# The last batch of a two-layer attention kernel: output products moved earlier, a flag tested earlier, a ScalarE table loaded earlier

## The chip, the cores and the metric

The kernel runs on one core of a Trainium2 chip. The core has five engines that run their own instruction streams and meet through semaphores: TensorE (PE in the profile, with its weight loads listed apart as PEld), VectorE (DVE), ScalarE (ACT), GpSimd (POOL) and SyncE (SP), which here issues most DMA transfers. The metric is device time in microseconds. All data are 32-bit floats; in the profile one 128x512 product of this kernel shows as two rows, each a weight load and a matmul.

## The reference, cut to what matters

The input x has shape 8 x 512 x 32 x 32: eight batches, 512 channels, 1024 positions. Two layers follow, each of the form "x plus attention of the group-normalised x". The change lies in the second layer, and almost all of it in its eighth and last batch:

```python
attn = jnp.einsum('bhdq,bhdT->bhqT', q, k) * scale
attn = jnp.einsum('gh,bhqT->bgqT', w_head, attn)      # mix the 8 heads
attn = jax.nn.softmax(attn, axis=-1)
attn = (attn - mean) / jnp.sqrt(var + EPS)            # over the whole map
attn = attn * in_gamma[None, :, None, None] + in_beta[None, :, None, None]
out = jnp.einsum('bhqT,bhdT->bhqd', attn, v)
out = out.reshape(b, t, c)
out = out @ w_proj.T + b_proj
```

## The kernel before, in words

**Second layer, one batch.** The class `Attention1` works through 8 blocks of 128 positions. `scores` (L1630) multiplies queries and keys into PSUM and ScalarE copies the result to `raw` (L1642). `regroup` (L1648, on SP's queue) moves `raw` into `re_t` by DMA so that the heads lie beside each other. `mix` (L1667) multiplies by the head weights into two PSUM tiles, and ScalarE takes the exponential of each (L1680). `flip` (L1695, VectorE) transposes it, `moments` (L1709, VectorE) takes the sums, and `values` (L1725) multiplies by the values. `leave` (L1741, ScalarE) copies the result into `out_view`, which has four blocks of 128 channels (`NCH` is 4), each made of two position blocks' results. `totals` (L1763 to L1783) gives the softmax divisors, which go through DRAM and come back spread over partitions as `rzb`; `divide` (L1810) multiplies a block by them. Blocks 0, 1 and 2 are divided by GpSimd during the steps, block 3 by VectorE in the tail.

**Order.** The order on PE, ACT, DVE, POOL and SP is written out by hand: inside `manual_schedule`, each engine runs its instructions in the order of the Python calls. `step(p, t, ag)` interleaves the work of block p (scores), p-1 (mix, flip) and p-2 (values). `ag` is an `Agenda`: a list of functions, each with a slot number, run when `step` reaches that slot. In the ninth step (p = 8, t = 0 to 3) no new scores are made. Slot 31.5 (`4 * NT - 0.5`) comes after the values and the copy of block 6's first half and just before `mix(7, 0)`.

**PSUM.** The pool `ps_m` has three tiles of two banks, used by scores, mixes and, in the tail, by the output products (`m_psum`); `ps_a` has two tiles of one bank (`acc_psum`).

**The tail.** After the ninth step `values(7, 0)` is finished, `values(7, 1)` follows, then `totals(3)`, `broadcast`, `instance` (variance terms of the normalisation) and `out1_last`. That function computes, for four output chunks `oc` of 128 channels and two halves `f` of 512 positions, the sum over four blocks `n` of weights times `out_view` (L1552; 32 products of 128x512 in all). For chunks 0 to 2 the blocks 0 to 2 come first and block 3 later; chunk 3 is done whole at the end (L1603). Between them stand `instance_end` (L1835 to L1847: scale A and offset cv), `divide(3)`, `check` (L1796 to L1803), the offset product (L1578), its sum `off` (L1582) and 32 ScalarE additions of `off` to x (L1589). Each output tile is then `ys = psum * A` (L1608), `ys + x` (L1613), and a DMA to DRAM (L1614).

**The flag.** At the very end VectorE reduces `chk` (L2024 to L2029), a matmul sums over partitions into `pflag` (L2031), VectorE compares and writes `flag` (L2033, L2034). Every engine loads the flag (L2038) and branches (L2039): if a softmax sum was out of range, the whole computation is run again in a general form (`general_path`); with these inputs the branch is taken past it. After that the engines meet and the program ends (L2088).

**The start.** ScalarE's first function is used at L864, where chunks 1 and 3 of the first batch are normalised (chunks 0 and 2 by VectorE, L862). The first products (L904) read these chunks.

Of the kernel before, what the change touches and what calls it, by code (L numbers as in the profile page):

```python
# [18 lines left out]
P = 128  # L19
# [5 lines left out]
Z_MAX, RZ_MAX = 1e17, 1e10  # L25
# [442 lines left out]
def tile_two_attention_layers(  # L468
# [47 lines left out]
    def const_tile(name, shape, dt=F32):  # L516
        return const.tile(shape, dt, tag=name, name=name)
# [751 lines left out]
    with ExitStack() as l1:  # L1269
# [10 lines left out]
        NCH = NT // 2  # L1280

        def acc_psum(nm):
            return ps_a.tile([P, FB], F32, tag="a", name=nm)
# [4 lines left out]
        def small_psum1(nm):  # L1288
            return m_psum(nm)[:, 0]
# [210 lines left out]
        def out_view(b):  # L1500


            return qo_t[b].rearrange("p (n two) a t -> p n (two a t)", two=2)
# [36 lines left out]
        def out1_last(a):  # L1540


            b = a.b
            w = w_t["p", b]
            tiles = {}

            def products(oc, blocks):
                if oc not in tiles:
                    tiles[oc] = m_psum(f"pp1_{b}_{oc}")
                for f in range(NFB):  # L1550
                    for n in blocks:
                        nc.tensor.matmul(  # L1552
                            tiles[oc][:, f], w[:, n, ts(oc, P)], out_view(b)[:, n, ts(f, FB)],
                            start=(n == 0), stop=(n == NCH - 1),
                        )

            last = NCH - 1

            x = rawpool.tile([P, NCC, T], F32, tag="raw", name="xs_last")
            for oc in range(NCC):  # L1560
                nc.sync.dma_start(out=x[:, oc], in_=x1_d[b][ts(oc, P), :])
            wsum = epool.tile([P, 2 * T], F32, tag="e", name="wsum")[:, :C]
            ys = etpool.tile([P, NCC, NFB, FB], F32, tag="et", name="ys_last")
            small = acc_psum("small_last")
            off = stat.tile([P, NCC, H], F32, tag="off", name="off", bufs=1)
            for oc in range(3):
                products(oc, range(last))
                if oc == 0:
                    nc.vector.tensor_add(wsum, w[:, 0], w[:, 1])
                    for n in range(2, NCH):  # L1570
                        nc.vector.tensor_add(wsum, wsum, w[:, n])
                    a.instance_end(small)
                    a.divide(last)
                    a.check()
                if oc == 1:
                    pc = small[:, H : H + NCC * H]
                    for o in range(NCC):
                        nc.tensor.matmul(  # L1578
                            pc[:, o * H : o * H + H], wsum[:, ts(o, P)], a.cv,
                            start=True, stop=True,  # L1580
                        )
                    nc.vector.tensor_add(  # L1582
                        off, pc.rearrange("p (c g) -> p c g", g=H),
                        pb1.unsqueeze(2).to_broadcast([P, NCC, H]),
                    )
                    for o in range(NCC):
                        for g in range(H):
                            xg = x[:, o, ts(g, P)]
                            nc.scalar.activation(  # L1589
                                xg, xg, AF.Identity, bias=off[:, o, g : g + 1]  # L1590
                            )
            halves = [acc_psum(f"pp1_last_{f}") for f in range(NFB)]
            h = FB // P
            for oc in range(NCC):
                if oc < last:
                    products(oc, [last])
                for f in range(NFB):
                    if oc < last:
                        ps = tiles[oc][:, f]
                    else:  # L1600
                        ps = halves[f]
                        for n in range(NCH):
                            nc.tensor.matmul(  # L1603
                                ps, w[:, n, ts(oc, P)], out_view(b)[:, n, ts(f, FB)],
                                start=(n == 0), stop=(n == NCH - 1),
                            )
                    y = ys[:, oc, f]
                    nc.vector.tensor_mul(  # L1608
                        y.rearrange("p (g t) -> p g t", t=P),
                        ps.rearrange("p (g t) -> p g t", t=P),  # L1610
                        a.A[:, f * h : f * h + h].unsqueeze(2).to_broadcast([P, h, P]),
                    )
                    nc.vector.tensor_add(y, x[:, oc, ts(f, FB)], y)  # L1613
                    nc.sync.dma_start(out=out_d[b, ts(oc, P), ts(f, FB)], in_=y)  # L1614

        class Attention1:
            def __init__(self, b):
# [239 lines left out]
            def step(self, p, t, ag):  # L1857
# [84 lines left out]
        for b in range(B):  # L1942
# [81 lines left out]
        nc.vector.tensor_reduce(top[:, 0:1], chk[:, 0], AX.X, ALU.max)  # L2024
        nc.vector.tensor_reduce(top[:, 1:2], chk[:, 1], AX.X, ALU.max)
        nc.vector.tensor_scalar(top[:, 0:1], top[:, 0:1], RZ_MAX, None, ALU.is_lt)
        nc.vector.tensor_scalar(top[:, 1:2], top[:, 1:2], Z_MAX, None, ALU.is_lt)
        good = stat.tile([P, 1], F32, tag="good", name="good")
        nc.vector.tensor_mul(good, top[:, 0:1], top[:, 1:2])  # L2029
        pf = small_psum1("pflag")  # L2030
        nc.tensor.matmul(pf[:, 0:1], ones, good, start=True, stop=True)  # L2031
        bad = stat.tile([P, 1], F32, tag="bad", name="bad")
        nc.vector.tensor_scalar(bad, pf[:, 0:1], P - 0.5, None, ALU.is_lt)  # L2033
        nc.vector.tensor_copy(flag, bad)  # L2034

    both.close()
    ordered.close()
# [54 lines left out]
```

## Time and profile before

| What | us |
|---|---|
| median of 3 runs | 3967.3 (3964.85 to 3968.17) |
| the profiled execution's own time | 3964.89 |
| its span, first to last instruction | 3963.1 |
| last `values(7, 1)` products begin (L1725) | 3913.68 |
| last output product row begins (L1603) | 3948.81 |
| last output sum ends (L1613) | 3950.92 |
| flag written (L2034) | 3952.46 |

PE is busy 98% of the span, DVE 70%, ACT 50%, POOL 4%. Times in the views are counted from the span's start. A line of a view names the code line, the engine, the operation, output <- input by tile name, and in brackets the idle time before it and what ended that. In a table of stretches each engine has its busy time and its number of instructions; PEclk is the share of full speed that PE's clock was granted.

### The profile page before, as it was taken

The page shows a single profiled execution, that of the slowest core. Times are in us where ns is not written, and L with a number is a line of the kernel's source. Part 1 is how long each engine was busy: PE and PEld are TensorE (multiplying, and loading weights), DVE is VectorE, ACT ScalarE, POOL GpSimd, SP SyncE. Part 2 cuts the span into 40 slices and gives each one's busy share as a digit, 9 for nine tenths or more (in the row PEclk, how much of TensorE's full clock was granted, in tenths as well). Part 3 has the DMA queues.
Part 4 walks back from the last instruction along what each step waited for, and adds up shares of the span by engine and source line. Part 5 has one row for each costly group of instructions (what it writes and reads, how often), then busy time and mean ns, then how long its engine had stood idle before and what let it go on. Part 6 is the DMA issues. An engine that isn't in the chain of part 4 may idle for free.

```text
span 3963.1 us, 95453 instructions
## 1 busy us (share of the span) xinstructions
PE 3874.9 (98%) x41868; PEld 1823.7 (46%) x41868; DVE 2769.6 (70%) x3741; ACT 1971.4 (50%) x2431; POOL 141.2 (4%) x182
## 2 busy tenths in 40 slices
PE   8999999999999999999999999999999999999997
PEld 4353535344353535344544545545545445445454
DVE  4747475665757474856967958859768679588596
ACT  1726354453627172624716718538347267175284
POOL 0000000000000000000100100001001001000010
PEclk9999999999999999999999999999999999999998
DMA  3313131121121121216938839749568478397494
GB/s 121 123 48 117 47 118 46 55 73 65 55 72 68 61 76 48 89 49 173 230 114 208 211 104 237 198 119 236 158 158 220 134 192 226 98 229 191 124 226 124
DMA packets 249593, 519.09 MB, mean 131 GB/s; under 512 B 51024, under 2 KB 58192, under 8 KB 242512
## 3 DMA queue, kind: packets, MB, share of 16 engines
q1 hardware_dynamic: 241984, 500.08, 44.2%
q0 software_dynamic: 7184, 12.81, 1.5%
q8 instruction: 331, 5.42, 0.6%
q14 instruction: 94, 0.77, 0.1%
HBM read 197.16 MB, written 46.92 MB: 62 GB/s over the span
## 4 chain that ended last, share of the span: by engine, by line
PE 90%; DVE 5%; DMA 3%; ACT 1%; issue 1%; SPq 0%; ACTq 0%; DVEq 0%
PE s L1086 11%; PE a L1112 11%; PE a L1725 11%; PE s L1630 10%; PE m L1667 6%; PE pk_p L904 6%; PE pq_p L904 5%; PE pv L1456 5%; PE pv_p L904 5%; PE pp_p L904 5%; PE pq L1381 4%; PE pp L1381 4%; PE pk L1381 3%; DMA re<-raw 3%; DVE et L1695 1%; DVE bn L1709 1%
## 5 line engine op out<-in xcount | busy, mean ns | idle before, releaser
L1695 DVE STREAM_TRANSPOSE et<-e 128x2048 f32<-128x2048 f32 x256 | 589.5, 2303 | 100.0 <-ACT e L1680 99.0
L1725 PEld LDWEIGHTS a<-et,v 128*64 128x64 f32 x16384 | 510.8, 139 | 296.4 <-issue 273.4
L1709 DVE BATCH_NORM_STATS2 bn<-e 128x6 f32<-128x512 f32 x1024 | 635.1, 681 | 0.0
L1091 ACT ACTIVATE e<-s 128x1024 f32<-128x1024 f32 x512 | 497.2, 1026 | 233.8 <-PE s L1086 233.4
L1642 ACT COPY raw<-s 128x1024 f32<-128x1024 f32 x480 | 470.2, 1018 | 211.6 <-PE s L1630 179.0
L1680 ACT ACTIVATE e<-m 128x1024 f32<-128x1024 f32 x512 | 496.3, 1021 | 156.1 <-issue 56.3
L1725 PE MATMUL a<-et,v 128*64 128x64 f32 x16384 | 558.9, 225 | 11.2 <-DVE et L1695 7.8
L1099 DVE TENSOR_TENSOR zacc<-zacc,e 128x1024 f32<-128x1024 f32 x384 | 468.7, 1221 | 87.8 <-ACT e L1091 65.5
L1630 PE MATMUL s<-k,q 64*64 64x512 f32 x4096 | 515.2, 607 | 5.8 <-DVE q L1496 3.2
L1086 PE MATMUL s<-q,k 64*64 64x512 f32 x4096 | 490.1, 593 | 2.3 <-ACT e L1091 2.3
L1112 PE MATMUL a<-e,v 64*64 64x512 f32 x4096 | 484.1, 589 | 0.0
L1667 PE MATMUL m<-re,wmix 32*32 32x512 f32 x8192 | 311.0, 602 | 19.5 <-DMA re<-raw 16.5
L1112 PEld LDWEIGHTS a<-e,v 64*64 64x64 f32 x4096 | 156.7, 133 | 282.8 <-issue 282.2
L1086 PEld LDWEIGHTS s<-q,k 64*64 64x64 f32 x4096 | 147.9, 133 | 275.2 <-issue 240.5
L1630 PEld LDWEIGHTS s<-k,q 64*64 64x64 f32 x4096 | 127.8, 132 | 220.8 <-issue 87.1
L1456 PE MATMUL pv<-wv,y 128*128 128x512 f32 x480 | 214.3, 599 | 0.0
L1773 POOL DMA_DIRECT2D zd<-rz x96 | 52.5, 552 | 3508.2 <-DVE rz L1767 3506.0
L1741 ACT COPY q<-a 64x256 f32<-64x256 f32 x256 | 94.0, 367 | 148.3 <-PE a L1725 146.2
L1456 PEld LDWEIGHTS pv<-wv,y 128*128 128x128 f32 x480 | 88.6, 190 | 119.8 <-issue 106.5
L1667 PEld LDWEIGHTS m<-re,wmix 32*32 32x32 f32 x8192 | 68.8, 103 | 162.4 <-ACT raw L1642 69.3
L1462 DVE COPY v<-pv 128x512 f32<-128x512 f32 x30 | 20.7, 689 | 159.5 <-PE pv L1456 80.9
L1097 DVE TENSOR_TENSOR zacc<-e,e 128x1024 f32<-128x1024 f32 x64 | 78.3, 1223 | 55.9 <-ACT e L1091 55.9
(317 smaller groups left out, 3866.4 us busy)
## 6 DMA issues: line engine op xcount, KB each, us to landing
re<-raw SPq DMA_DIRECT2D x1024, 256.0 KB
left_q<-left_q SPq DMA_DIRECT2D x17, 1792.0 KB
left_p<-left_p SPq DMA_DIRECT2D x17, 1792.0 KB
left_k<-left_k SPq DMA_DIRECT2D x10, 1792.0 KB
x<-in_x_dram SPq DMA_DIRECT2D x32, 512.0 KB
rzb<-zd SPq DMA_DIRECT2D x128, 128.0 KB
x<-x SPq DMA_DIRECT2D x64, 256.0 KB
y<-x SPq DMA_DIRECT2D x32, 512.0 KB
```

The lines of the kernel that those rows point to most:

```text
L904: nc.tensor.matmul(out, st, mv, start=start, stop=(k == 1), skip_group_check=True)
L1086: nc.tensor.matmul(ps[c * D : c * D + D, m], k[r, hp, k0 : k0 + D], q[r, hp, ts(f, FB)], start=True, stop=True,)
L1091: nc.scalar.activation(e[i], ps, AF.Exp, scale=S0 * S0)
L1112: nc.tensor.matmul(acc[g][a][m * D : m * D + D], v[rows, kc, ts(2 * hp + m, D)], e[i][rows, m], start=(kc == 0), stop=(kc == NG - 1),)
L1456: nc.tensor.matmul(ps[:, m], y_t[b][:, c, ts(2 * i + m, P)], w[:, c], start=(c == 0), stop=(c == NCC - 1),)
L1630: nc.tensor.matmul(ps[c * D : c * D + D, m], qo_t[b][r, p, hp, ts(c, D)], k_t[b][r, hp, ts(kh, FB)], start=True, stop=True,)
L1642: nc.scalar.copy(dst, ps)
L1667: nc.tensor.matmul(ps[a // 2][c * 32 : c * 32 + 32, a % 2].rearrange("p (r h k) -> p h r k", r=2, h=2), wmix[rows].rearrange("p g i -> p ( ...
L1680: nc.scalar.activation(e[:, :, 2 * h : 2 * h + 2].rearrange("p r a k -> p a r k"), ps[h].rearrange("p a (r k) -> p a r k", r=2), AF.Exp,)
L1695: nc.vector.transpose(self.et[p, u].rearrange("p kb (r st a) g q -> p st kb r (a g q)", r=2, st=2)[:, st], self.e[p, s].rearrange("p r a ( ...
L1709: nc.vector.bn_stats(self.bn[n][:, p % 2, s, a], e[:, :, a].rearrange("p r k -> p k r"))
L1725: nc.tensor.matmul(acc[two * D : two * D + D, s].rearrange("p (x q) -> p x q", q=4), v_t[b][:, kb, ts(g, D)], et[:, kb, :, g], start=(kb = ...
```

## The change

Three edits:

1. `out1_last` is cut in two. It now returns `products` and `rest`. A function `prelude` in slot 31.5 of the last batch calls it and runs `products(0, [0, 1])`: four 128x512 products. After `leave(7, 0)`, ahead of `values(7, 1)`, come `products(0, [2])` and `products(1, [0, 1])`: six more. `products` skips what has been done. The rest of the tail keeps its order, without these ten products.
2. The test of the sums becomes `set_flag`, called after `off` and the products of chunk 2's first three blocks, ahead of the last results. Its matmul writes to the tile `small_last` in place of one from `ps_m`. In the built program SP's load of the flag stands ahead of the eight output transfers; on the other engines it stays after their last work.
3. A one-column ScalarE `Identity` into a new tile `first_act` stands early in the program, so ScalarE's table load comes before L864. The tile takes 32 bytes of each partition ahead of `chk`, so in the built program all SBUF tiles allocated later lie 32 bytes higher.

```diff
+    first_act = const_tile("first_act", [P, 1])
+    nc.scalar.activation(first_act, ones[:, :1], AF.Identity)
     chk = const_tile("chk", [P, 2, NCHK])
...
-            tiles = {}
+            tiles, done = {}, set()
             def products(oc, blocks):
+                blocks = [n for n in blocks if (oc, n) not in done]
+                done.update((oc, n) for n in blocks)
                 if oc not in tiles:
                     tiles[oc] = m_psum(f"pp1_{b}_{oc}")
...
+            def rest():
...
+                for oc in range(3):
+                    products(oc, range(last))
...
+                set_flag(small)
+                halves = [acc_psum(f"pp1_last_{f}") for f in range(NFB)]
...
+            return products, rest
...
+        def set_flag(pf):
+            top = stat.tile([P, 2], F32, tag="top", name="top")
+            nc.vector.tensor_reduce(top[:, 0:1], chk[:, 0], AX.X, ALU.max)
+            nc.vector.tensor_reduce(top[:, 1:2], chk[:, 1], AX.X, ALU.max)
+            nc.vector.tensor_scalar(top[:, 0:1], top[:, 0:1], RZ_MAX, None, ALU.is_lt)
+            nc.vector.tensor_scalar(top[:, 1:2], top[:, 1:2], Z_MAX, None, ALU.is_lt)
+            good = stat.tile([P, 1], F32, tag="good", name="good")
+            nc.vector.tensor_mul(good, top[:, 0:1], top[:, 1:2])
+            nc.tensor.matmul(pf[:, 0:1], ones, good, start=True, stop=True)
+            bad = stat.tile([P, 1], F32, tag="bad", name="bad")
+            nc.vector.tensor_scalar(bad, pf[:, 0:1], P - 0.5, None, ALU.is_lt)
+            nc.vector.tensor_copy(flag, bad)
...
+                def prelude():
+                    out_products.extend(out1_last(a))
+                    out_products[0](0, [0, 1])
+                out_products = []
+                ag.at(4 * NT - 0.5, prelude)
...
                 a.values(last, 0, 2, 3)
                 a.leave(last, 0)
+                out_products[0](0, [2])
+                out_products[0](1, [0, 1])
                 a.values(last, 1, 0, 1, 2, 3)
                 a.leave(last, 1)
                 a.totals(NCH - 1)
                 a.broadcast(1)
                 a.instance()
-                out1_last(a)
+                out_products[1]()
...
-        top = stat.tile([P, 2], F32, tag="top", name="top")
...
-        pf = small_psum1("pflag")
-        nc.tensor.matmul(pf[:, 0:1], ones, good, start=True, stop=True)
```

More of the change, by code (lines that the diff above doesn't have):

```diff
@@ L1557, in out1_last @@
             last = NCH - 1
[L1559 to L1580, printed above, removed]
-                        )
[L1582 to L1597, printed above, removed]
-                    if oc < last:
[L1599 to L1614, printed above, removed]
+            def rest():
+                x = rawpool.tile([P, NCC, T], F32, tag="raw", name="xs_last")
+                for oc in range(NCC):
+                    nc.sync.dma_start(out=x[:, oc], in_=x1_d[b][ts(oc, P), :])
+                wsum = epool.tile([P, 2 * T], F32, tag="e", name="wsum")[:, :C]
+                ys = etpool.tile([P, NCC, NFB, FB], F32, tag="et", name="ys_last")
+                small = acc_psum("small_last")
+                off = stat.tile([P, NCC, H], F32, tag="off", name="off", bufs=1)
+                for oc in range(3):
+                    products(oc, range(last))
+                    if oc == 0:
+                        nc.vector.tensor_add(wsum, w[:, 0], w[:, 1])
+                        for n in range(2, NCH):
+                            nc.vector.tensor_add(wsum, wsum, w[:, n])
+                        a.instance_end(small)
+                        a.divide(last)
+                        a.check()
+                    if oc == 1:
+                        pc = small[:, H : H + NCC * H]
+                        for o in range(NCC):
+                            nc.tensor.matmul(
+                                pc[:, o * H : o * H + H], wsum[:, ts(o, P)], a.cv,
+                                start=True, stop=True,
+                            )
+                        nc.vector.tensor_add(
+                            off, pc.rearrange("p (c g) -> p c g", g=H),
+                            pb1.unsqueeze(2).to_broadcast([P, NCC, H]),
+                        )
+                        for o in range(NCC):
+                            for g in range(H):
+                                xg = x[:, o, ts(g, P)]
+                                nc.scalar.activation(
+                                    xg, xg, AF.Identity, bias=off[:, o, g : g + 1]
+                                )
+                set_flag(small)
+                halves = [acc_psum(f"pp1_last_{f}") for f in range(NFB)]
+                h = FB // P
+                for oc in range(NCC):
+                    if oc < last:
+                        products(oc, [last])
+                    for f in range(NFB):
+                        if oc < last:
+                            ps = tiles[oc][:, f]
+                        else:
+                            ps = halves[f]
+                            for n in range(NCH):
+                                nc.tensor.matmul(
+                                    ps, w[:, n, ts(oc, P)], out_view(b)[:, n, ts(f, FB)],
+                                    start=(n == 0), stop=(n == NCH - 1),
+                                )
+                        y = ys[:, oc, f]
+                        nc.vector.tensor_mul(
+                            y.rearrange("p (g t) -> p g t", t=P),
+                            ps.rearrange("p (g t) -> p g t", t=P),
+                            a.A[:, f * h : f * h + h].unsqueeze(2).to_broadcast([P, h, P]),
+                        )
+                        nc.vector.tensor_add(y, x[:, oc, ts(f, FB)], y)
+                        nc.sync.dma_start(out=out_d[b, ts(oc, P), ts(f, FB)], in_=y)
@@ L2021, in tile_two_attention_layers @@
             q_projection(b + 1).run()
-        top = stat.tile([P, 2], F32, tag="top", name="top")
[L2024 to L2029, printed above, removed]
-        pf = small_psum1("pflag")
-        nc.tensor.matmul(pf[:, 0:1], ones, good, start=True, stop=True)
-        bad = stat.tile([P, 1], F32, tag="bad", name="bad")
-        nc.vector.tensor_scalar(bad, pf[:, 0:1], P - 0.5, None, ALU.is_lt)
-        nc.vector.tensor_copy(flag, bad)
     both.close()
```

## The prediction

> **What bounds the kernel now.** PE is busy 98% of the span, so I read the chain of work that ended last first, for the last 50 us. Columns: start, length, what.
>
> ```profile
> 3913.68 6.23 PE a L1725 x128
> ...
> 3920.33 5.35 PE pp L1552 x12
> ...
> 3932.13 10.40 PE pp L1552 x24
> 3942.53 6.88 PE pp_last L1603 x16
> ...
> 3950.23 0.69 DVE ys_last L1613
> ...
> 3952.31 0.15 DVE flag L2034
> ```
>
> From 3913.68 to 3949.4 PE is the chain; then come the last output sum and the test of the flag. Next, where PE stands still before that (timeline; in brackets the idle time and what ended it):
>
> ```profile
> 3894.01 1.34 PE L1667 MATMUL m<-re,wmix 32*32 32x512 f32 x32 [3.82 <-DMA re<-raw]
> ...
> 3913.68 6.23 PE L1725 MATMUL a<-et,v 128*64 128x64 f32 x128 [5.34 <-DVE et L1695]
> ```
>
> Two holes, 3.82 and 5.34 us. The second is VectorE's: from 3897.40 it flips and sums without a pause until 3916.2. The 128 products after it take 6.23 us, while 128 of the same kind from 3904.38 take 3.95. The stretches tell why (stretch, length, PE, PEld, DVE, ACT, POOL busy, PEclk):
>
> ```profile
> 3894.85:3898.26 3.41, 3.41 (x80) 2.06 (x64) 0.86 (x1) 1.94 (x2) 0.00 (x0) 0.50 0.73 194
> 3898.26:3908.40 10.14, 10.07 (x317) 7.53 (x288) 10.14 (x11) 6.04 (x8) 0.00 (x0) 1.00 0.01 3
> ...
> 3911.92:3918.74 6.82, 5.06 (x95) 5.09 (x97) 4.25 (x6) 0.00 (x0) 0.00 (x0) 0.50 0.01 2
> ```
>
> After each hole PE's clock is halved, in steps of 3.41 us. Last, the code lines of the flag's branch and of the end:
>
> ```profile
> L2039 POOLq EVENT_SEMAPHORE  x5: 17/43/43, 3956.3 to 3956.6; - x5
> L2039 PEldq COMPARE_BRANCH  x1: 4335/4335/4335, 3953.1 to 3953.1; - x1
> L2039 DVEq EVENT_SEMAPHORE  x1: 21/21/21, 3956.6 to 3956.6; - x1
> L2039 POOLq INC_SWDGE_SEM  x1: 1237/1237/1237, 3956.7 to 3956.7; - x1
> L2088 POOLq DRAIN  x3: 46/103/4315, 3957.9 to 3962.8; - x3
> ```
>
> The flag is written at 3952.46, each engine loads it (0.5 us) and branches at 3953.1; then 3.2 us pass before POOL goes on, 3.5 before DVE, 4.3 for PE. POOL then does 1.24 us and a drain of 4.32, until 3962.26; the engines meet and the span ends at 3963.1. From the last sum's end (call it A, 3950.92) to the end are 12.2 us.
>
> [...] worked out from the matmul records, windows in which PE was busy 25, 42, 46 and 49% were followed by half clock, those with 50 and 59% not. [...]
>
> **Part 1: ten products moved.** A row of a 128x512 product takes 0.429 us (15 rows from 3942.37 to 3948.81), a product two rows.
>
> Prelude: 4 products are 8 rows, 3.43 us. PE comes free at 3890.20 and the mix's data come at 3894.0, so it ends at 3893.7: hidden, with 0.3 us to spare. The weights and blocks 0 and 1 have long been there (last division of block 1: 3849.8 to 3852.1); its PSUM tile was freed at 3887.2. If the cover were gone, 3.43 us would fall on the mix and VectorE's run. The window is now over half busy, so the mix runs at full clock: 1.15 instead of 1.34 us. VectorE's run, which starts when its exponentials are done, moves 0.2 us ahead.
>
> The prelude keeps one of three `ps_m` tiles. So each later mix waits for both exponentials of the mix before: mix 1 at 3897.2 (before 3897.19), mix 2 at 3900.4 (3899.85), mix 3 at 3904.0 (3903.21). Queued behind them on PE are the values. The exponentials of mixes 2 and 3 wait for VectorE's sums (to 3901.9 and 3906.5), so the run isn't delayed: cost 0. PE's holes there are below 1 us in each window. Values(7,0) ends at 4.0+1.15+3.95 past 3900: 3909.1 instead of 3908.33.
>
> Six products: 12 rows, 5.15 us, to 3914.3. VectorE's last flip ends at 3913.35, so values(7,1) starts 0.6 us later than before, but at full clock: 3.95 instead of 6.23. With the divisors' 0.55 us PE is done at 3918.75, not 3920.33: 1.58 gained.
>
> Tail: what is late next is VectorE. Before, PE had 5.35 us of products while VectorE made `isb`; now nothing. `isb` takes 2.40 us from there (3920.33 to 3922.73): 3921.15. Then PE: `instance_end` 0.35, two products 1.72, to 3923.3. VectorE has the weights' sum ahead (2.1 us, to 3923.2), then 2.99 us to `cv`: 3926.25. So PE stands 2.4 and 2.95 us. Then 8 offset rows 0.79; 12 rows 5.15; the flag's matmul 0.2; 12 rows 5.15, to 3937.6; the last of 16 rows starts 6.44 later, 3944.05, and A follows as before (3948.81 to 3950.92) after 2.1: 3946.15. So A comes 4.77 us earlier. Division 3 waits for `rzb`, 8.8 us behind the divisors: 3927.9 to 3929.1, ahead of its use at 3932.5. `off` then waits for `check`, to 3930.0; ScalarE's 9.45 us end at 3939.9, its first chunk at 3932.8, in time for the sums from 3934.2.
>
> The two holes in the tail can halve the clock. Sliding the 3.41 us window over them: in some 60% of positions a window under half busy leaves the next halved, 1.7 us lost; in the others nothing. Mean 1.0. Before, the hole of 5.34 lost 2.5 us in this profile (5.06 us at half clock), and 1.7 as a mean over positions: so 0.8 of the gain is this profile's.
>
> **Part 2: the flag.** VectorE's 7 short operations (1.5 us with waits) leave the end; in their new place five end by 3930.9, inside its idle time, and the last two wait for PE at 3932.5, ahead of the first output at 3933.5. SP loads the flag ahead of the eight output DMAs (0.48+0.19+0.03, to 3934.0); its first DMA is due at 3934.9. POOL has nothing left to do, so its load, fetch, 1.24 us and drain of 4.32, 10 us in all, lie under the products. ACT's lie there too. Then DVE ends last: its queue runs ahead of its data path (the step for L1571's second sum stands at 3923.4, while the first, begun at 3923.4, runs 0.69), so it loads the flag during the last sum: A-0.6, +0.55, +0.08, +3.47 is A+3.5, then SP's and POOL's meeting, 1.15: A+4.65. If it loads only after the sum: A+5.4. PE, whose last row starts at A-2.1, needs 0.5+4.4: A+2.8. The last output landed 1.7 us after A. So 12.2 becomes 4.65 to 5.4: 6.8 to 7.5 gained; I take 7.3.
>
> **Part 3: the table.** It saves ScalarE 1.28 us ahead of chunk 1. But see:
>
> ```profile
> 20.65 8.84 PE L904 MATMUL pk_p<-n,left_k 128*128 128x512 f32 x16 [4.39 <-DVE n L862]
> 21.00 2.37 ACT L864 ACTIVATE n<-x,nn,scale 128x1024 f32<-128x1024 f32 x2
> ...
> 24.37 0.59 ACT L928 COPY tmp<-pk_p 128x512 f32<-128x512 f32 x1 [1.00 <-PE pk_p L904]
> 26.09 0.59 ACT L928 COPY tmp<-pk_p 128x512 f32<-128x512 f32 x1 [1.13 <-PE pk_p L904]
> ```
>
> PE starts on VectorE's chunk 0; four rows end at 24.3 (3.7 us), the next four take 1.72: the first are at half clock, two of them cover 20.65 to 22.36, and chunk 1 is there at 22.19. From there PE runs without a hole to 33 us. Worth 0 to 0.2; without that cover 1.2. I take 0.1.
>
> **Sum.** 4.77+7.3+0.1-1.0 = 11.2 against the profile's 3964.9: 3953.7. The runs' median is 2.4 above it; from there, without this profile's 0.8, 3967.3-10.4 = 3956.9. I take 3956.
>
> **Rivals.**
> (a) The end doesn't shrink: POOL's drain of 4.32 us waits for the others and starts after them. For it: nothing else in the trace ends with it. Against: its start at 3957.95 follows POOL's own step directly, and it outlasts SP's last step (3958.67). Then the flag's 1.55 is all of part 2: 5.5 us less gain, 3961.5.
> (b) The clock takes the gain: holes of 2.4 and 2.95 us, plus short ones between the mixes, halve two or three windows, 3.4 to 5.1 us instead of 1.0. Against: PE is over 65% busy in every mix window. 3958.5 to 3960.
> (c) Slower: the 32 bytes. [...] The chain has 3% of the span, 119 us, in `re<-raw` transfers[...]. It decides from 9% (10.7 us); to be slower by 0.2% it needs 16%, giving 3975. Against: PE waits for these transfers only 15 times, 16.5 us.
>
> **Chances.** Forecast 0.72, (a) 0.12, (b) 0.10, (c) 0.06. A measurement of this kernel can tell about 0.2%, 7.9 us, from no change: 3959.4. Forecast and half of (b) are faster, 0.77; (a) and the rest 0.17 the same; (c) 0.06 slower. Range 3951 to 3961.5: below by a tail without lost windows and a table worth 1.2, above by (b) and up to (a); (c) is left out.
>
> **What would show it.** Right: prelude rows between 3890.2 and 3893.7 with the mix near 3894.0; values(7,1) in about 3.95 us; two PE holes of 2 to 3 us in the tail, ended by `isb` and `icv`; POOL's drain over before the last outputs; last sum to end of span 4.6 to 5.4 us; PE's first row still at 20.65. Wrong: the mix late by the prelude, the drain after DVE's branch, or a changed duration in the rows that the change doesn't touch.

## The result, and the profile after

The changed kernel takes 3956.1 us (median of 22 runs, 3949.9 to 3966.3), the kernel before 3965.2 us in the runs beside it (22, 3959.1 to 3969.3). The ratio is 0.9981, 95% interval 0.9975 to 0.9987: 7.5 us less, 5.2 to 9.9 (the two medians lie 9.1 us apart, within that interval). It is faster, by about as much as can be told from no change. The profiled execution took 3957.81 us, its span is 3956.0 us. (The line numbers of the tail are 4 to 9 higher than before, those of the end 19.)

The chain of work that ended last, its last part (start, length, what):

```profile
3912.11 5.35 PE pp L1556 x12
3917.46 3.88 PE a L1734 x128
...
3924.09 0.69 DVE wsum L1575
...
3929.17 1.30 PE small_last L1584 x8
3930.47 6.69 PE pp L1556 x12
...
3942.54 6.88 PE pp_last L1610 x16
...
3950.24 0.69 DVE ys_last L1620
```

The products now stand ahead of the last values, which take 3.88 us, and the flag has left the end of the chain. In the middle the chain has gone over to VectorE (from the divisors at 3921.8 to `icv` at 3929.1). The twelve product rows after that take 6.69 us, where the twelve at 3912.11 take 5.35.

PE's holes, from the timeline (in brackets the idle time and what ended it):

```profile
3892.90 3.70 PE L1556 MATMUL pp<-q,left_p 128*128 128x512 f32 x8
3896.98 1.15 PE L1676 MATMUL m<-re,wmix 32*32 32x512 f32 x32 [0.38 <-DMA re<-raw]
...
3912.04 5.42 PE L1556 MATMUL pp<-q,left_p 128*128 128x512 f32 x12
3917.39 3.95 PE L1734 MATMUL a<-et,v 128*64 128x64 f32 x128
...
3924.32 0.36 PE L1844 MATMUL small_last<-isb,ones 64*128 64x8 f32 x2 [2.54 <-DVE isb L1835]
...
3929.17 1.30 PE L1584 MATMUL small_last<-icv,wsum 128*128 128x8 f32 x8 [2.59 <-DVE icv L1856]
```

The prelude fills the first hole but for 0.38 us, and the mix still starts when its data come. The hole of 5.34 us ahead of the last values is gone. Two holes stand in the tail instead. The stretches of the clock's 3.41 us around the second (stretch, length, busy time and count of PE, PEld, DVE, ACT and POOL, PEclk, DMA share, GB/s):

```profile
3926.42:3929.83 3.41, 0.82 (x7) 0.66 (x6) 2.29 (x15) 0.00 (x0) 0.00 (x0) 1.00 0.77 185
3929.83:3933.24 3.41, 3.41 (x8) 1.86 (x8) 2.37 (x10) 0.14 (x1) 0.00 (x0) 0.50 0.99 374
```

PE was busy for 0.82 of 3.41 us, and the next 3.41 us ran at half clock: this is the only such stretch in the last 2000 us of the changed kernel's profile ahead of the end; the one before had three there, one of them of 6.83 us.

The code lines of the flag's branch and of the end:

```profile
L2058 POOLq COMPARE_BRANCH  x1: 50/50/50, 3938.3 to 3938.3; - x1
L2058 POOLq INC_SWDGE_SEM  x1: 1232/1232/1232, 3941.2 to 3941.2; - x1
L2058 PEldq COMPARE_BRANCH  x1: 3992/3992/3992, 3942.3 to 3942.3; - x1
L2058 DVEq COMPARE_BRANCH  x1: 76/76/76, 3950.9 to 3950.9; - x1
L2058 DVEq EVENT_SEMAPHORE  x1: 21/21/21, 3954.1 to 3954.1; - x1
L2107 POOLq DRAIN  x3: 46/103/4315, 3942.5 to 3955.7; - x3
```

POOL branches at 3938.3, and its drain of 4.32 us runs from 3942.5 to 3946.8, under the products. The fetch that the prediction counts for POOL is the time from its branch to its next step: 3.2 us before (3953.07 to 3956.26), 2.6 here (3938.26 to 3940.82). The instruction queues moved 5 packets (0.05 MB) from 3953 to 3956.5 before, and 4 (0.03 MB) from 3938 to 3942.5 here; that they set its length isn't shown. DVE still branches at the last output sum's end (A, 3950.93), and goes on 3.2 us later; SP branches at 3951.3, behind its last output transfer. From A to the end of the span are 5.1 us instead of 12.2.

Three distances split the last 60 us so that they can be compared between profiles whatever came earlier: from the start of the mix, `mix(7, 0)`, to the end of the divisors' last product (z), from z to A, and from A to the end. The starts, ends and clock records come from each kernel's trace:

| Kernel | mix to z | z to A | A to end | half clock after z |
|---|---|---|---|---|
| before | 26.32 | 30.60 | 12.2 | 0 |
| flag only | 27.44 | 30.82 | 4.8 | 0 |
| table only | 26.19 | 30.60 | 12.6 | 0 |
| changed | 24.80 | 29.15 | 5.1 | 3.41 |
| changed, again | 24.80 | 30.55 | 5.1 | 10.24 |
| products only | 24.82 | 27.25 | 12.5 | 3.41 |
| products only, again | 24.80 | 30.69 | 12.3 | 10.24 |
| changed, GpSimd late | 24.80 | 29.92 | 10.3 | 10.24 |
| changed, prelude twice | 24.81 | 30.81 | 4.8 | 10.24 |
| changed, with filler | 24.80 | 27.48 | 5.2 | 0 |
| prelude only | 26.50 | 28.05 | 5.3 | 0 |
| six only | 24.80 | 31.08 | 4.9 | 6.83 |
| other order of the tail | 24.80 | 24.36 | 4.8 | 0 |
| other order, ScalarE's share | 24.80 | 23.08 | 4.9 | 0 |

### The profile page after: what moved, and what is told of

The parts are those of the page before. It is cut to its first block, busy times and chain, and to the rows that moved or that the text cites. A ratio compares the mean times of both kernels' runs of the same rounds, so it can differ in the third digit from the quotient of the medians.

```text
span 3956.0 us, 95453 instructions
## 1 busy us (share of the span) xinstructions
PE 3873.6 (98%) x41868; PEld 1820.5 (46%) x41868; DVE 2770.1 (70%) x3741; ACT 1970.7 (50%) x2432; POOL 140.9 (4%) x182
## 3 DMA queue, kind: packets, MB, share of 16 engines
q8 instruction: 331, 5.42, 0.6%
```

## The experiments

Runs of one kernel scatter by 3 us (standard deviation) before the change and by 4 us after it, so a ratio from some 20 runs has an interval of about 2.5 us to each side. Effects of 1 to 2 us are read in the table above, and the ratios only say whether the sum agrees.

### The flag alone

The kernel before, with the removed block at the end turned into `set_flag` and called here:

```diff
+            set_flag(small)
             halves = [acc_psum(f"pp1_last_{f}") for f in range(NFB)]
```

> The kernel before with the flag's test alone moved ahead of the last results (in the tile small_last); no products moved, no early table load. Theory (the end shrinks because every engine's load of the flag and its branch, POOL's drain above all, lie under the products): last output sum to end of span 4.6 to 5.4 us instead of 12.2, the tail's products unchanged but for one matmul of 0.2 us (PE free before the mix to last output sum 60.7 to 61.0 us), so 7.0 us less, ratio about 0.9982. Rival (most of what the changed kernel gains comes from the products, the flag gives only its own 1.55 us): ratio 0.9996.

Measured: 0.9982 (0.9975 to 0.9988, 21 runs), 7.1 us less. A to the end is 4.8 us. PE free to A (from PE's last values ahead of the mix to the last output sum) is 62.25 us (3884.77 to 3947.02), 1.25 more than the upper value expected. z to A is unchanged (30.82 against 30.60), so the excess lies ahead of z: in this profile two stretches of 6.83 us at half clock fell there, against 3.41 and 6.83 before. The flag is worth what the theory says; the rival's 1.55 us is out. Its 7.1 us are also as much as the runs show for the whole change (7.5 us, and 6.7 in a second comparison below): that the ten products add to it has to be read from the stages.

### The products alone, twice

The changed kernel with the flag's test put back to the end and `first_act` taken out:

```diff
-    first_act = const_tile("first_act", [P, 1])
-    nc.scalar.activation(first_act, ones[:, :1], AF.Identity)
...
-                set_flag(small)
```

> The kernel before with the ten products moved alone; the flag is tested at the end as before, no early table load. Theory: last output sum to end of span stays 12.2 us; from PE coming free before the mix to the last output sum 56 to 58 us instead of 60.7, depending on whether a tail hole costs a window at half clock; 2.7 to 4.8 us less, ratio 0.9988 to 0.9993. Rival (the clock takes the gain: two or more windows at half clock in the tail): 60 us and ratio 0.9998 to 1.0. Rival (the products give all of the gain): ratio 0.9976.

Measured: 0.9998 (0.9990 to 1.0006, 13 runs). PE free to A: 55.70 us (3883.64 to 3939.34), even less than expected; A to the end 12.5. The tail had gained 5 us in the profile and the runs next to nothing, so the kernel was run again:

> The same kernel as the run with the products moved alone, once more: in its profile the time from the mix's start to the last output sum was 52.1 us against 56.9 before, while its runs were as long as those of the kernel before (0.9998, 0.9990 to 1.0006, from 13 runs). Theory (the gain in the tail is real and the first comparison of runs scattered high): from the mix's start to the last output sum 52 to 54.5 us again, ratio 0.9988 to 0.9995. Rival (something outside the tail takes the gain back in this build): the same tail and ratio 0.9998 or more.

Measured: 0.9990 (0.9984 to 0.9997, 21 runs), 4 us less. But mix to A was 55.49 us here, and not 52 to 54.5: z to A is 30.69, as long as before the change. The stretches of the clock after z show why:

```profile
3922.66:3926.07 3.41, 1.67 (x5) 0.97 (x6) 3.24 (x7) 0.00 (x0) 0.00 (x0) 1.00 0.08 2
3926.07:3929.48 3.41, 1.30 (x3) 0.23 (x2) 2.69 (x17) 0.00 (x0) 0.00 (x0) 0.50 0.53 143
3929.48:3932.89 3.41, 3.41 (x11) 2.38 (x12) 1.50 (x3) 0.00 (x0) 0.00 (x0) 0.50 0.91 333
3932.89:3936.31 3.42, 3.42 (x6) 1.35 (x5) 0.69 (x6) 2.59 (x9) 0.00 (x0) 0.50 0.73 292
```

The stretch with the hole at `isb` (PE busy 1.67 of 3.41 us) is followed by one at half clock. That one holds the hole at `icv` (PE busy 1.30 us), and the clock stays at half; the one after (3.41 us busy, 11 matmuls) holds the eight offset products of eight columns each, and it stays at half again. Three stretches in a row, not one. The two comparisons give 0.8 and 4.0 us, 2.4 on average, half of the 4.8 that the tail can give at full clock. That something outside the tail takes the gain back isn't shown: the repetition is faster than the kernel before by its whole interval.

### The prelude alone, and six products alone

Prelude only: the changed kernel without

```diff
-                out_products[0](0, [2])
-                out_products[0](1, [0, 1])
```

> The changed kernel without the six products ahead of the last values: only the four of the prelude are moved; flag and table as changed. Theory (after the divisors VectorE's chain to isb and icv takes 7.4 us whatever PE does, so products left in the tail fill PE's holes there): a hole of 4 to 5.3 us ahead of the last values returns, the holes at isb and icv fall to 0.7 us and nothing; from the mix's start to the last output sum 52.0 to 54.5 us against 53.95 in the changed kernel, ratio 0.9978 to 0.9984. Rival (each product moved is worth its 0.86 us): 59 us, ratio 0.9993.

Six only: the prelude's products taken out, and chunk 0's first three blocks ahead of the last values:

```diff
-                    out_products[0](0, [0, 1])
...
-                out_products[0](0, [2])
-                out_products[0](1, [0, 1])
+                out_products[0](0, [0, 1, 2])
```

> The changed kernel without the prelude; the six products ahead of the last values are chunk 0's blocks 0 to 2. Theory (as for the prelude alone): a hole of 3.5 to 4.5 us ahead of the first mix returns, with one or two windows at half clock after it; none ahead of the last values; a hole of 2.4 us at isb, none at icv; from the mix's start to the last output sum 52.7 to 55.3 us, ratio 0.9978 to 0.9984. Rival (each product moved is worth its 0.86 us): 57.4 us, ratio 0.9989.

Measured: prelude only 0.9987 (0.9981 to 0.9994, 21 runs), just above the range expected, mix to A 54.55 us, at its edge; six only 0.9983 (0.9976 to 0.9990, 19 runs), mix to A 55.88. The timeline of the first:

```profile
3916.44 6.50 PE L1734 MATMUL a<-et,v 128*64 128x64 f32 x128 [4.44 <-DVE et L1704]
...
3925.90 0.36 PE L1844 MATMUL small_last<-isb,ones 64*128 64x8 f32 x2 [0.62 <-DVE isb L1835]
3926.18 5.42 PE L1556 MATMUL pp<-q,left_p 128*128 128x512 f32 x12
3931.44 0.95 PE L1584 MATMUL small_last<-icv,wsum 128*128 128x8 f32 x8
```

And of the second:

```profile
3896.91 2.02 PE L1676 MATMUL m<-re,wmix 32*32 32x512 f32 x32 [4.13 <-DMA re<-raw]
...
3924.25 0.56 PE L1844 MATMUL small_last<-isb,ones 64*128 64x8 f32 x2 [2.54 <-DVE isb L1835]
3924.75 8.24 PE L1556 MATMUL pp<-q,left_p 128*128 128x512 f32 x12
```

With the prelude alone, products left in the tail fill both of its holes: 0.62 us at `isb`, none at `icv`, no half clock, z to A 28.05 us. With six alone the half clock after the hole at `isb` takes another 2.8 us (12 rows in 8.24 us instead of 5.42), which put mix to A 0.6 us above the expected range. Neither is near what "each product moved is worth 0.86 us" asks for (59 and 57.4 us, 0.9993 and 0.9989), though neither ratio can tell the two: both intervals hold the rival's value. The profiles can. What is moved out of the tail earns only what the tail doesn't give back in holes and clock. Mix to z is 24.80 with six alone too: the mix at half clock starts VectorE's run 0.9 us later (first flip 4.18 us after the mix's start instead of 3.30), which the six products still cover. So with the six in place the prelude shortens nothing up to z.

### The holes filled with products for nothing

Four more products into a spare PSUM tile, whose result is never read, two at `isb` and two at `icv`:

```diff
+                        filler(2)
                         a.instance_end(small)
+                        filler(2)
                         a.divide(last)
```

> The changed kernel with four more 128x512 products whose result is never read, two in PE's hole at isb and two in its hole at icv; nothing else. Theory (the holes themselves cost nothing more than VectorE's chain, but they halve the clock of the products behind them): no stretch at half clock in the tail, from the divisors' last product to the last output sum 27.2 to 27.9 us, against 27.3 to 30.7 in the profiles without the filler; about 2 us faster than the changed kernel, ratio lower by 0.0003 to 0.0007. Rival (the tail's spread has another cause, the transfers of x and of the divisors): 29 to 31 us in spite of a full clock, ratio the same as the changed kernel's or higher.

Beside it, on the same chip, the changed kernel itself:

> The changed kernel itself, once more, beside the next three. Theory: 24.8 us from the mix's start to the divisors' last product; from there to the last output sum 27.3 us if no stretch at half clock falls on the products, up to 31 us if three do; last output sum to end 4.8 to 5.3 us; ratio 0.9978 to 0.9986.

Measured: with filler 0.9980 (0.9969 to 0.9992, 10 runs), the changed kernel 0.9983 (0.9976 to 0.9990, 21 runs). The ratios can't be told apart, the profiles can: with filler z to A is 27.48 us at full clock, and without it 30.55 us with three stretches at half clock (mix to z 24.80 in both). The filler's timeline:

```profile
3919.74 1.98 PE L1576 MATMUL filler<-q,left_p 128*128 128x512 f32 x4
3922.34 0.35 PE L1855 MATMUL small_last<-isb,ones 64*128 64x8 f32 x2 [0.62 <-DVE isb L1846]
3922.63 1.98 PE L1576 MATMUL filler<-q,left_p 128*128 128x512 f32 x4
3924.45 1.88 PE L1556 MATMUL pp<-q,left_p 128*128 128x512 f32 x4
3927.21 1.06 PE L1595 MATMUL small_last<-icv,wsum 128*128 128x8 f32 x8 [0.88 <-DVE icv L1867]
```

The offset product starts 7.40 us after z (3919.81), as in the changed kernel (3929.17 after 3921.78: 7.39). So the holes as such cost nothing beyond VectorE's chain, and by these two profiles what stood between 27.5 and 30.5 us is the clock behind them.

### The prelude's products twice

```diff
+                    out_products[0](0, [0, 1], True)
                     out_products[0](0, [0, 1])
```

(`True`: computed, and computed again by the second call.)

> The changed kernel with the prelude's four products done twice, the first time for nothing: 6.9 us of products in place of 3.4 in the hole ahead of the first mix. Theory (the hole, 3.6 to 5.3 us in all profiles so far, covers 3.4 us of products but not 6.9): from PE's last values to the mix 7.0 to 7.2 us and no wait for the transfer, the mix 1.8 to 3.4 us late, 24.8 us from the mix to the divisors as before, 2 to 3 us slower than the changed kernel, ratio higher by 0.0004 to 0.0008. Rival (the prelude's products are hidden at any length, since VectorE's run is what counts): the mix late, but VectorE's first flip no later and the same ratio.

Measured: 0.9989 (0.9981 to 0.9997, 14 runs) against 0.9983 for the changed kernel beside it, some 2.4 us more, within the intervals of both. Its timeline:

```profile
3891.44 7.13 PE L1557 MATMUL pp<-q,left_p 128*128 128x512 f32 x16
3898.50 1.14 PE L1677 MATMUL m<-re,wmix 32*32 32x512 f32 x32
...
3901.82 2.31 DVE L1705 STREAM_TRANSPOSE et<-e 128x2048 f32<-128x2048 f32 x1 [6.00 <-ACT e L1690]
```

The mix starts 7.06 us after the prelude does and waits for nothing. VectorE stood for 6.00 us ahead of its run, where it stood for 3.00 in the changed kernel:

```profile
3900.28 2.31 DVE L1704 STREAM_TRANSPOSE et<-e 128x2048 f32<-128x2048 f32 x1 [3.00 <-ACT e L1689]
```

That the prelude's products are hidden at any length is out by this profile: in the others the mix starts 3.6 to 5.3 us after PE's last values, and what is longer comes on top.

### GpSimd kept busy to the end

```diff
+                late = stat.tile([P, 1], F32, tag="late", name="late", bufs=1)
+                nc.gpsimd.tensor_copy(late, ys[:, NCC - 1, NFB - 1, :1])
```

> The changed kernel with one small GpSimd copy of a column of the last output into an unused tile, so that GpSimd cannot load the flag, branch and drain before the last output sum. Theory (the drain was the end and is now covered by the products): last output sum to end of span 10.2 to 11.5 us instead of 5.05, 5.2 to 6.4 us slower than the changed kernel, ratio to the kernel before about 0.9995. Rival (VectorE's own late load and branch set the end in any case and the drain counts for little): 5.1 to 6.5 us, ratio 0.9981 to 0.9984.

Measured: A to the end 10.3 us, 5.2 more than in the changed kernel. The code lines of its flag and end:

```profile
L2060 POOLq COMPARE_BRANCH  x1: 50/50/50, 3947.1 to 3947.1; - x1
L2060 DVEq EVENT_SEMAPHORE  x1: 21/21/21, 3949.4 to 3949.4; - x1
L2060 POOLq INC_SWDGE_SEM  x1: 1237/1237/1237, 3950.4 to 3950.4; - x1
L2109 POOLq DRAIN  x3: 46/103/4315, 3951.6 to 3956.5; - x3
```

DVE is through at 3949.4, but POOL branches only at 3947.1, after its copy; 2.9 us later it goes on, and its drain holds the end until 3956.0. The drain was the end of the kernel before, and the products now cover it. The runs say more than that: 1.0008 (0.9999 to 1.0017, 13 runs, 3954 to 3978 us), some 10 us slower than the changed kernel, twice what the end explains. The clock doesn't explain it (z to A is 29.92 us, between the changed kernel's 29.15 and 30.55). It stays open, with runs that scatter by 6 us and a profile taken in one of the faster ones (3958.59).

### The table alone

```diff
+    first_act = const_tile("first_act", [P, 1])
+    nc.scalar.activation(first_act, ones[:, :1], AF.Identity)
     chk = const_tile("chk", [P, 2, NCHK])
```

> The kernel before with the early ScalarE function and its tile alone, so that the table is loaded early and all later tiles lie 32 bytes higher. Theory (two products at half clock cover ScalarE's late chunk, and the shift costs nothing): PE's first product row at 20.6 to 20.9 us, ScalarE's first copy of a product at 24.3 to 24.7 us, ratio 0.9995 to 1.0005. Rival (the table's 1.28 us come out of the start): the first copy at 23.1 us, ratio 0.9997 with everything behind it 1.2 us earlier. Rival (the shift makes the transfers slower): 1.0006 to 1.003 and longer waits on the transfers from raw to re.

Measured: 1.0003 (0.9995 to 1.0011, 14 runs). The table's load takes 1.28 us and stood at 19.70 before (at 0.75 in the changed kernel's profile). The start:

```profile
19.53 2.38 ACT L866 ACTIVATE n<-x,nn,scale 128x1024 f32<-128x1024 f32 x2 [17.28 <-DVE nn L813]
20.46 9.24 PE L906 MATMUL pk_p<-n,left_k 128*128 128x512 f32 x16 [4.38 <-DVE n L864]
...
24.25 0.59 ACT L930 COPY tmp<-pk_p 128x512 f32<-128x512 f32 x1 [2.34 <-PE pk_p L906]
```

ScalarE's chunk is done 1.3 us sooner after `nn`, but it then waits 2.34 us for PE instead of 1.00: its first copy comes at 24.25 (before 24.37), with PE's first row at 20.46 (before 20.65). PE's weight loads there follow each other at 0.85 us (21.45, 22.30, 23.16, 24.01), later at 0.43 (24.82, 25.25, 25.68). The table is worth nothing. With the shift by 32 bytes the transfers take a little longer: the packets of SP's queue took 44.2, 44.4, 44.5 and 44.2% of the engines' time in the four profiles without it, and 44.4 to 44.7% in the ten with it: by the means (44.33 and 44.55) 0.5% more (that share is of all of the queue's transfers, not of the rows of `raw` alone). A time for it can't be told: the interval reaches from 2 us faster to 4.4 slower.

### Another order in the tail

The same work; the products left in the tail stand where PE has its holes, `check` with another scratch tile and `off` come ahead of the last division, and chunk 3 is begun before block 3 is divided:

```diff
+                products(1, [2])
+                products(2, [0])
...
                 a.instance_end(small)
+                a.check(re_t[:64, NF + 3, 1])
+                products(2, [1, 2])
...
+                last_chunk(0, range(last))
+                set_flag(small, lambda: a.divide(last))
```

> The changed kernel with another order in the tail: chunk 1's block 2 and chunk 2's block 0 ahead of the variance product, chunk 2's blocks 1 and 2 ahead of the offset product, the offset sum ahead of the last division, chunk 3's first half begun before the last blocks; the same work. Theory (the two tail holes of 2.5 us on PE, and the half clock that follows them, are the rest of what is to be had there): both holes under 0.5 us, no stretch at half clock in the tail, from PE coming free before the mix to the last output sum about 52 us instead of 58.0 (56.3 without a lost window), then VectorE's eight output pairs of 1.39 us become what sets the end; 4 to 6 us faster than the changed kernel, ratio to the kernel before 0.9963 to 0.9972. Rival (the holes are hidden by VectorE's output pairs in any case, or the holes move elsewhere): 0 to 1.5 us faster than the changed kernel, ratio 0.9977 to 0.9981.

Measured: 0.9976 (0.9969 to 0.9983, 21 runs), 9.5 us less than the kernel before. The two stages of its profile, mix to z and z to A:

```profile
3901.45:3926.25 24.80, 24.46 (x531) 15.69 (x531) 18.76 (x21) 9.47 (x14) 0.37 (x1) 1.00 0.15 36
3926.25:3950.61 24.36, 20.83 (x57) 9.47 (x56) 20.23 (x56) 9.81 (x33) 0.00 (x0) 1.00 0.55 185
```

No half clock, and 24.36 us from z to A: 4.8 us less than in the changed kernel's first profile and 6.2 less than in its second, as expected. (PE free to A was 54.5 us, not 52; 1.2 us of the difference are the mix's data, which came 5.3 us after PE was free and not 4.0.) The ratio gains less than forecast, some 2 us over the changed kernel, and the intervals overlap. VectorE's eight output pairs run from 3939.39 to A without a pause, 11.2 us, and are the bound now. So one more step, with x loaded (`out_products[2]`) ahead of the last values and chunk 3 scaled by ScalarE:

```diff
+                out_products[2]()
                 out_products[0](0, [2])
...
+                            for g in range(f * h, f * h + h):
+                                nc.scalar.activation(
+                                    ys[:, oc, f, ts(g - f * h, P)], ps[:, ts(g - f * h, P)],
+                                    AF.Identity, bias=off[:, oc, g : g + 1], scale=a.A[:, g : g + 1],
+                                )
```

> The tail in the other order, with x loaded ahead of the last values instead of behind the divisors' transfers, and chunk 3's two halves scaled and offset by ScalarE from PSUM in place of VectorE's product (ScalarE's eight additions of the offset for that chunk fall away). Theory (in the other order VectorE's eight output pairs behind the last division are the bound, and x's load delays the divisors' transfer): from the divisors' last product to the last output sum 22 to 23.2 us against 24.4 in the other order alone, no stretch at half clock; 1 to 2 us faster than the other order, 5 to 7 us faster than the changed kernel; ratio to the kernel before 0.9962 to 0.9972. Rival (the last division's data come no earlier and ScalarE's four operations are slower than VectorE's one): 24 to 25 us.

Measured: 0.9969 (0.9958 to 0.9980, 7 runs), 12 us less than the kernel before; the changed kernel beside it has 0.9983 (0.9976 to 0.9990). z to A is 23.08 us. The timeline:

```profile
3931.22 1.23 DVE L1833 TENSOR_TENSOR q<-q,rzb 128x1024 f32<-128x1024 f32 x1
...
3942.77 1.51 ACT L1630 ACTIVATE ys_last<-pp_last,off,iA 128x128 f32<-128x128 f32 x4 [1.93 <-PE pp_last L1603]
```

The division starts 9.3 us after z (3921.93) and waits for nothing, where it waited for its data until 9.8 us after z in the other order (3936.09 after 3926.25), and ScalarE's four operations lie beside VectorE's sums. What each of the two steps is worth by itself wasn't run. In the profiles both orders beat both kernels; in the runs they beat the kernel before by their whole intervals, and the changed kernel only by the middle of theirs.

## Why the prediction came out right

The time, 3956, was met, and partly by luck: the kernel before ran 2 us faster in these comparisons (3965.2) than in the first three runs (3967.3), and the gain was 7.5 us by the ratio (6.7 in the second comparison) where 11.3 had been forecast from the median.

- **The prelude** is hidden with 0.38 us to spare (forecast 0.3), and holds up the mix when doubled. Right, but by a narrow margin: of the nine profiles with one prelude, the mix waits for its data behind it in seven (0.38 to 1.62 us); in two (changed, again; products only) it follows the prelude at once, and whether it was held up there stays open.
- **The mix at full clock** moves VectorE's run ahead by 0.1 us (forecast 0.2: from mix to first flip 3.39 before, 3.30 after). With the flag alone and with the table alone, the first flip comes 4.17 us after the mix's start, so there it would be 0.9. The waits for the exponentials (0.18 and 0.17 us) delay nothing. Right.
- **The six products.** Values at full clock in 3.95 us; mix to z 24.80 us in every kernel that has them, 26.2 to 27.4 in the three with no product moved: 1.9 us on average (forecast 1.58). Right; the 0.8 us that the forecast then took off, as a slow clock that only its own profile had, was not there to take off: that profile's 26.32 is no longer than the average of the three.
- **The tail.** The holes are as forecast: 2.54 and 2.59 us (forecast 2.4 and 2.95). The clock is the step that failed: "in some 60% of positions a window under half busy leaves the next halved, 1.7 us lost; in the others nothing. Mean 1.0." In the six profiles with the change's own order after z, four had three stretches at half clock in a row, and only two had one. z to A was 27.25 us at its best and 29.73 on average, so the clock took 2.5 us and not 1.0. The step counted each hole by itself. In the four, stretches at half clock with the second hole (PE busy for 1.30 to 2.83 of 3.41 us) or with eight-column products (2.83 to 3.42) were followed by half clock again. So this part gave 0.9 us (30.67 on average in the three kernels with no product moved) where 3.2, less 1.0 for the clock, had been forecast. Rival (b), two or three windows at half clock, had been given 0.10; it came in four of these six profiles, three stretches each, at 2.7 to 3.6 us more than the 27.25, where the rival had up to 5.1 for three.
- **The flag.** 12.4 to 5.0 us on average (four profiles with the flag late, nine with it early): 7.4 gained, forecast 7.3. DVE branches at A and goes on at A+3.2 (forecast A+3.5), with SP beside it. Rival (a) is out: POOL's drain follows POOL's own step, under the products (from 3942.5) or, where that is late, behind them (GpSimd late, from 3951.6).
- **The table** is worth nothing: PE's first four rows, two products, take 3.7 us where the next four take 1.72, and cover ScalarE's chunk. The clock's records of the profile before begin only at 24.14 us, so the half clock there is read from these times. Right (forecast 0.1).
- **Rival (c)**: what the shift could cost was an estimate that no run had shown. The transfers took 0.5% more (44.33 to 44.55% of the engines' time), and no loss in time could be told.

The sum of the stages, 1.9 + 0.9 + 7.4 = 10.2 us, stands against 10.4 forecast from the median, and that is luck too: the tail gave 1.3 us less than its share, the stage ahead of z 1.1 more (1.9 where 1.58 less 0.8 had been counted). But the runs show 7.5 and 6.7 us, with intervals that end at 9.9 and 9.5. Each stage rests on single executions, and what the 3 us are, scatter or a small loss elsewhere such as (c)'s, stays open. The parts compared by their runs give 7.1 us for the flag and 2.4 for the products, less 1.2 for the table and the shift: 8.3. Since the flag alone is as fast in the runs as the whole change, the gain of the flag is shown by profiles and runs, and that of the products on top of it (2.8 us by the stages) by the profiles alone.

## What to carry to other kernels

When work is moved out of a stage to fill a hole elsewhere, see what it was hiding where it stood: here the products had covered VectorE's chain, and without them PE's clock fell (to 0.50 in one to three stretches of 3.41 us). Place the products that remain in the new holes first, before moving more. What an engine still has to do behind a late branch or flag was hidden here by letting the engines that are done early reach it early (7.4 us).

## What the runs showed of the hardware

**Stretches of eight-column products were followed by half clock.** In the kernel before, in the timeline far ahead of the change:

```profile
1822.71 3.48 PE L1474 MATMUL pvs<-ys,wv 128*64 128x8 f32 x114
```

PE is busy without a pause, and at 1826.38 the clock is halved. The two stretches of the clock there:

```profile
1822.96:1826.38 3.42, 3.42 (x116) 3.34 (x116) 0.15 (x1) 0.01 (x1) 0.00 (x0) 1.00 0.98 242
1826.38:1829.79 3.41, 3.41 (x20) 1.05 (x16) 0.08 (x1) 1.15 (x2) 0.00 (x0) 0.50 1.05 252
```

The same products stand in all 14 profiles. In ten of them a stretch of 3.41 us at full clock fell on them, PE busy throughout with 108 to 124 matmuls, and the next was at half clock each time. By the matmul records these products took 94% of that stretch before, and all of it in the changed kernel.

**The bound of the prediction isn't sharp.** It came from the profile before alone (25 to 49% busy, half clock; 50 and 59%, not), and left out the stretch shown above. In the profiles before and after, from 100 us to A, the stretches at full clock with PE busy for 0, 24, 25, 42 and 46% were followed by half clock, and of those with 50% and more only the two filled by eight-column products. With the flag alone one with 53% (1.80 of 3.41 us, from 1802.17) was followed by half clock as well.

**At half clock, more than half busy wasn't enough.** After stretches at half clock with PE busy for 38 to 76% the full clock didn't come back (38% products only, again; 44% prelude twice; 48% before; 66% prelude only; 69 and 70% flag only; 76% changed, again). Where it did, PE had been busy for 82 to 100% (82% products only; 83% six only; 88 and 89% table only). Six further stretches, with 82 to 100%, stayed at half. Two of these hold the products of 8 columns at `isb`, 0.56 us of them (six only, 82%; GpSimd late, 90%); without that time they would stand at some 65 to 75%, by my estimate. The other four have 10 or 11 matmuls, where the stretch from 3932.89 above, as busy and also at half clock, has 6: I take it that the eight offset products are in them. That such products count for little at half clock is argued from this, not shown by itself.

**PE's queue ran ahead.** PE's load of the flag and its branch (3942.3, 3.99 us) are over at 3946.3, before its last row starts (3948.81), and so in no one's way (the prediction had PE's branch end at A+2.8). SP's step at 3954.04, which I take for its wait for the last output transfer, comes 3.1 us after A, nearly as late as DVE's at 3954.11: in this profile the end has two holders, and to shorten one alone would gain next to nothing. No run tried it.
